# A selective scan cut into tiles of 32 channels x 4 states instead of 64 x 2, with the state sums issued as four 32-column matmuls

## The chip, the cores and the metric

The kernel runs on one core of one Trainium2 chip. A core has five engines that run beside each other[...]: TensorE (PE in the profile, with PEld for its weight loads), VectorE (DVE), ScalarE (ACT), GpSimd (POOL) and SyncE (SP), which here issues most of the DMAs. Each works through its own list of instructions in order. The metric is the device time of one execution in microseconds (us). Times given for the kernel before are the median of three runs, and one further execution was recorded by the profiler.

## The reference

The input is a batch of 8 images of 64 channels and 64 x 64 pixels, in fp32. Four layers follow each other:

- layer 0: attention of all 4096 pixels over each other, a depthwise 3x3 convolution and 1x1 convolutions;
- layer 1: two blocks of window attention (8 x 8 windows, 8 heads) with their MLPs;
- layer 2: a filter that depends on position and image, and a 1x9 convolution;
- layer 3: a selective scan in four directions, then a gated sum of pooled convolutions.

The change is in the scan of layer 3. For every image, each of four directions k, each of 128 channels c and each of 16 states n, with L = 4096 time steps:

```python
def step(h, inp):
    u_t, dt_t, B_t, C_t = inp
    h = h * jnp.exp(dt_t[..., None] * A) + dt_t[..., None] * B_t[:, :, None, :] * u_t[..., None]
    return (h, jnp.einsum('bkcn,bkn->bkc', h, C_t))
```

So each (channel, state) has a first-order recurrence over time, and the output of a channel is the sum over its 16 states of h times C. B and C depend on the state and on time, not on the channel; dt and u depend on the channel and on time, not on the state.

## The kernel before, in words

**Pairs and streams.** The images are handled in four pairs p. For a pair, `front` computes layers 0 to 2 and the sources of the scan (the inputs of the four directions and the gate, written to DRAM), `scans` computes the scan, and `back` does the closing work (normalisation, output projection, pooled convolutions). The front of the first pair runs alone. After that, `scans(p)` runs with `back(p - 1)` and then `front(p + 1)` beside it: these are generators that yield their nominal cost, and after each step of the scan the loop advances them by a share in proportion. With the last pair only `back(2)` and, near its end, `back(3)` are left to stand beside the scan. A scheduler then sets the order of the instructions in each engine's list, within the dependencies; `net.behind` adds one more constraint on order without a semaphore.

**Units and steps.** A unit is one image, one direction and one chunk of 512 time steps (TD); a pair has 64 units. A unit has 128 x 16 = 2048 recurrences of 512 steps. A tile has 128 partitions, so it takes 16 tiles. Before the change a tile holds 64 channels x 2 states (GRP = 2), and a step of the scan handles two tiles (j = 0, 1, the two halves of the channels) with the same two states. A unit has 8 steps.

For each unit, one unit ahead:

- `load` fetches the input xs from DRAM;
- `inputs` computes dt (a matmul into `pdd`, then Exp and Ln on ACT) and the 32 rows of B and C (a matmul into `pbc`), and writes these rows to a DRAM tile `rows`;
- `spread` computes dt times u on DVE (L1735) and spreads dt and dt times u over the states by DMAs from SBUF to SBUF into `du` (L1739): one DMA for each of GRP groups of 128 / GRP channels, each channel's row written to GRP partitions. There are two `du` buffers.

For each step i:

- `fetch` (L1746) brings two rows of B (three steps ahead) and two rows of C (two steps ahead), each row spread over 64 partitions; 256 KB each, four buffers each;
- `products` (L1754, two steps ahead) multiplies B with dt u on POOL into a `vd` buffer of two tiles; there are eight `vd` buffers;
- `step` computes for both tiles the decay `dad` = Exp(dt A) on ACT (L1776) into a PSUM bank, runs the recurrence on DVE (`tensor_tensor_scan`, L1779) into an SBUF tile `hd` or in place into `dad`, keeps the last column for the next chunk on ACT (`carry`, L1787), and multiplies with C into `vd` again: tiles in `hd` on POOL (L1790 both tiles, L1793 one), tiles in `dad` on DVE (L1793). How many of the two tiles DVE takes (`own`) depends on the stage: none and one in turn, or, beside the attention and in the last pair, one, and two at every fourth step. There are two `hd` buffers for even steps and two for odd ones;
- `sums` adds up over the states on PE (L1805): a matmul with the constant `fold` takes the 128 partitions of a tile to 64 channels. The two tiles go to the two halves of the partitions of one PSUM bank `yd`, in which all 8 steps of the unit accumulate. The table `DUE` says after which step a step's sums are issued; it leaves out the step at which `yd` is read;
- `gather` on DVE (L1818 to L1823) adds the finished `yd` into Y at step 2 of the next unit.

All fetches, the spreading DMAs and the loads and stores of the scan stand in one list, SP's.

**Other places that the change touches**, for room in SBUF or with it: `normed` (the buffer `n_sd`), the attention's `e` buffers (L1306), the tile `t1` of layer 2 (L1579 to L1581), and `ge` in the closing work (L1899 to L1902).

Of the kernel before, what the change touches and what calls it, by code (L numbers as in the profile page):

```python
# [9 lines left out]
F32 = mybir.dt.float32  # L10
# [7 lines left out]
P = 128  # L18
# [8 lines left out]
GRP = 2  # L27
# [1132 lines left out]
class _Direct:  # L1160
# [69 lines left out]
    def normed(self, wk, srcs, cen, avg, eps, out_view=None):  # L1230
# [9 lines left out]
        sd = wk.tile([P, CH], F32, name="n_sd", tag="n_sd")  # L1240
# [24 lines left out]
    def layer0(self, p):  # L1265
# [11 lines left out]
        with self.work("w0") as wk:  # L1277
# [10 lines left out]
            for jc in range(NCH):  # L1288
# [9 lines left out]
                for t in range(32):  # L1298
# [6 lines left out]
                    for im in range(2):  # L1305
                        e = wk.tile([P, CH], F32, name="e", tag="e", bufs=6)  # L1306
# [228 lines left out]
    def layer2(self, X):  # L1535
# [11 lines left out]
        with tc.tile_pool(name="w2", bufs=2) as wk:  # L1547
            net.load(wk, (5,))
            cf = net.channel_filters(X, wk, self.pf, "f")
            for c in range(NCH):  # L1550
# [106 lines left out]
    DUE = ((-2,), (-2,), (), (-3,), (-3, -2), (-2,), (-2,), (-2,))  # L1657

    def scans(self, p, beside, cost):
# [39 lines left out]
        for i in (n - 2, n - 1):  # L1699
            self.sums(i, steps[i])  # L1700
# [40 lines left out]
    def fetch(self, i, st, s):  # L1741

        n = NST * s + 2 * (i % 8)
        t = st["BC"[s]] = self.sw.tile([P, TD], F32, name="BC"[s], tag="BC"[s], bufs=4)
        row = self.units[i // 8]["rows"][n : n + 2]
        self.nc.sync.dma_start(t, row.unsqueeze(0).to_broadcast([64, 2, TD]))  # L1746
# [5 lines left out]
    def products(self, i, st):  # L1752
        v = st["v"] = self.sw.tile([P, 2, TD], F32, name="vd", tag="v", bufs=8)
        self.nc.gpsimd.tensor_tensor(v, self.twice(st["B"]), self.units[i // 8]["du"][:, :, 1], ALU.mult)  # L1754

    def step(self, i, st):
# [14 lines left out]
        h = wk.tile([P, 2 - i % 2, TD], F32, name="hd", tag=f"h{i % 2}", bufs=2)  # L1771
        hs = []
        for j in range(2):
            n = n0 + j
            da = self.bank("dad", (P, TD), "da")
            nc.scalar.activation(da, u["du"][:, j, 0], AF.Exp, scale=net.As[:, k, n : n + 1])  # L1776
# [19 lines left out]
    def sums(self, i, st, after=None):  # L1796

        nc, w, net = self.nc, self.w, self.net
        wk, ps = self.sw, self.ps
        u = self.units[i // 8]  # L1800
        k, c = u["k"], u["c"]
        if i % 8 == 0:
            u["y"] = ps.tile([P, TD], F32, name="yd", tag="y", bufs=1)
        for j in range(2):
# [152 lines left out]
```

## Time and profile before

| what | value |
|---|---|
| median of three runs | 12742.49 us (12727.7 to 12745.85) |
| the profiled execution | 12767.64 us |
| its span in the trace | 12765.8 us |
| DMA queue of the scan | 754752 packets, 1510.30 MB, 39.4% of 16 engines' span |
| B and C fetches | 2048 each, 256 KB, 3.6 and 3.5 us from issue to landing |
| du DMAs | 512 of 512 KB, 5.9 us from issue to landing |
| one product on POOL (two tiles) | 2371 ns |
| one scan on DVE | 1267 ns into hd, 1273 ns into dad |
| one decay on ACT | 682 ns |
| one pass of a sum on PE | 738 ns, two passes a matmul, 8192 passes |

How it is read: "busy" is the time in which an engine had an instruction at work. Several of PE's passes can be at work at once, so the mean time of one is more than its share of the time. A group of instructions carries the line of the source and the tiles it writes and reads, as `yd<-vd,pack`. After a group stands the idle time of its engine just ahead of it and what ended that wait. A stretch of the span can be asked for by itself; its row has the length, the busy time and number of PE, PEld, DVE, ACT and POOL, the granted share of the clock of TensorE, the mean busy share of the DMA engines, and GB/s. A row of waits has who waited for whom, the total in us, how many times, and the longest. SPq is the list of DMAs that SP issues.

The stages follow each other in the trace like this: the first pair's front alone up to about 1815 us; the scans of the pairs from there to about 4550, 7475, 10405 and 12520; then the last closing work to the end. Beside the first three scans stand, in this order, the closing work of the pair before (not in the first), the attention of layer 0 of the next pair, its depthwise convolution, its layer 1, its layer 2 and the preparing of its scan's sources.

### The profile page before, as it was taken

How to read it: one execution, taken by the hardware profiler on the slowest of the kernel's cores; microseconds unless marked ns; L12 is line 12 of the kernel's file. 1: busy time of each engine (PE TensorE's matmuls, PEld its weight loads, DVE VectorE, ACT ScalarE, POOL GpSimd, SP SyncE). 2: the span in 40 equal slices, each digit the busy share in tenths (PEclk: the TensorE clock that was granted, in tenths of full speed). 3: DMA queues.
4: the chain of work that ended last, by engine and by line, in shares of the span. 5: the costliest groups of instructions: out<-in, count | busy, mean ns of one | idle time of the engine just before them, and what ended most of it. 6: DMA issues, size and time to landing. Idle time of an engine off the chain costs nothing. (4 is left out here: it accounts for less than half of the span.)

```text
span 12765.8 us, 142485 instructions
## 1 busy us (share of the span) xinstructions
PE 9843.7 (77%) x46358; PEld 3333.1 (26%) x46358; DVE 8687.9 (68%) x10259; ACT 7009.2 (55%) x15693; POOL 7550.7 (59%) x3844
## 2 busy tenths in 40 slices
PE   9888879987887667997888756997888855555556
PEld 2255222223342112222443211222433211111111
DVE  0122256777786776668776679467777679998878
ACT  5533247765663655665665555665566365455444
POOL 0000026677776683667776676467777567777874
PEclk9966779997888778998888877998888967777667
DMA  0000024544443462444443454344444356556554
GB/s 19 1 1 1 6 98 145 150 146 133 133 128 111 145 189 81 138 140 145 125 131 113 128 176 144 93 140 142 126 134 129 100 174 183 170 165 186 171 172 123
DMA packets 779703, 1575.84 MB, mean 123 GB/s; under 512 B 89280, under 2 KB 89408, under 8 KB 778176
## 3 DMA queue, kind: packets, MB, share of 16 engines
q1 hardware_dynamic: 754752, 1510.30, 39.4%
q10 hardware_dynamic: 24192, 56.32, 1.2%
q8 instruction: 367, 6.01, 0.2%
q14 instruction: 392, 3.21, 0.1%
HBM read 1197.16 MB, written 100.66 MB: 102 GB/s over the span
## 5 line engine op out<-in xcount | busy, mean ns | idle before, releaser
L1754 POOL TENSOR_TENSOR vd<-B,du 128x1024 f32<-128x1024 f32 x2048 | 4821.4, 2371 | 3295.1 <-DMA B<-rows 2016.1
L1805 PE MATMUL yd<-vd,pack 128*64 128x512 f32 x8192 | 2946.2, 738 | 933.7 <-POOL vd L1793 595.3
L1776 ACT ACTIVATE dad<-du,As 128x512 f32<-128x512 f32 x4096 | 2733.8, 682 | 1122.5 <-DVE vd L1793 458.5
L1779 DVE TENSOR_TENSOR_SCAN hd<-dad,carry,vd 128x512 f32<-128x512 f32 x1992 | 2497.0, 1267 | 480.0 <-ACT dad L1776 324.4
L1793 POOL TENSOR_TENSOR vd<-hd,C 128x512 f32<-128x512 f32 x1290 | 1659.8, 1290 | 1046.7 <-DVE hd L1779 1030.0
L1779 DVE TENSOR_TENSOR_SCAN dad<-dad,carry,vd 128x512 f32<-128x512 f32 x1592 | 2004.8, 1273 | 166.6 <-ACT dad L1776 164.4
L1790 POOL TENSOR_TENSOR vd<-hd,C 128x1024 f32<-128x1024 f32 x491 | 1158.1, 2359 | 735.5 <-DVE hd L1779 406.6
L1307 ACT ACTIVATE e<-s 128x512 f32<-128x512 f32 x2048 | 1200.2, 591 | 628.3 <-PE s L1301 626.5
L1301 PE MATMUL s<-X 64*128 64x512 f32 x4096 | 1435.8, 646 | 79.6 <-ACT e L1307 58.8
L1805 PEld LDWEIGHTS yd<-vd,pack 128*64 128x64 f32 x8192 | 667.0, 160 | 2815.0 <-issue 1214.6
L1793 DVE TENSOR_TENSOR vd<-dad,C 128x512 f32<-128x512 f32 x1824 | 1207.5, 673 | 239.6 <-ACT carry L1787 232.0
L1293 PE MATMUL po<-e,VT 128*64 128x512 f32 x4096 | 1207.8, 623 | 16.9 <-ACT e L1307 10.2
L1459 PEld LDWEIGHTS w_av<-vals,wide 64*64 64x64 f32 x16384 | 678.1, 173 | 209.7 <-ACT wide L1449 106.3
L1459 PE MATMUL w_av<-vals,wide 64*64 64x9 f32 x16384 | 705.6, 224 | 34.8 <-ACT wide L1449 34.6
L1787 ACT ACTIVATE carry<-hd 128x1 f32<-128x1 f32 (+1 forms) x1559 | 307.6, 200 | 697.1 <-DVE hd L1779 681.0
L1301 PEld LDWEIGHTS s<-X 64*128 64x128 f32 x4096 | 393.4, 186 | 1107.5 <-issue 832.6
L1787 ACT ACTIVATE carry<-dad 128x1 f32<-128x1 f32 x1594 | 268.1, 168 | 698.3 <-DVE dad L1779 688.9
L1717 PE MATMUL pdd<-xs,xdt 128*128 128x512 f32 x512 | 375.7, 824 | 334.6 <-issue 103.1
L1444 DVE TENSOR_TENSOR wide<-w_s,bias 128x512 f32<-128x512 f32 x512 | 327.7, 680 | 254.5 <-PE w_s L1431 246.5
L1449 ACT ACTIVATE wide<-wide 128x512 f32<-128x512 f32 x512 | 309.5, 626 | 318.7 <-DVE wide L1444 194.3
L1239 PE MATMUL pv<-n_sq,pack 128*128 128x512 f32 x576 | 364.5, 718 | 144.0 <-ACT n_sq L1237 130.0
L1316 DVE COPY att<-po 128x512 f32<-128x512 f32 x32 | 21.7, 679 | 643.3 <-PE po L1293 643.3
(246 smaller groups left out, 11137.5 us busy)
## 6 DMA issues: line engine op xcount, KB each, us to landing
B<-rows SPq DMA_DIRECT2D x2048, 256.0 KB, 3.6
C<-rows SPq DMA_DIRECT2D x2048, 256.0 KB, 3.5
du<-du SPq DMA_DIRECT2D x512, 512.0 KB, 5.9
xs<-xt SPq DMA_DIRECT2D x128, 256.0 KB, 3.6
xs<-xc SPq DMA_DIRECT2D x128, 256.0 KB, 3.8
xc<-xcv ACTq DMA_DIRECT2D x64, 256.0 KB, 2.1
zs<-z ACTq DMA_DIRECT2D x64, 256.0 KB, 3.8
xt<-XT ACTq DMA_DIRECT2D x32, 512.0 KB, 4.6
```

Of the source, the lines that this page charges most:

```text
L1293: nc.tensor.matmul(po[half[im]], lhsT=VT[:, t, half[im]], rhs=es[im], start=(t == 0), stop=(t == 31))
L1301: nc.tensor.matmul(ss[im], lhsT=at(half[im], t), rhs=X[half[im], jc * CH : (jc + 1) * CH], start=True, stop=True)
L1307: nc.scalar.activation(e, ss[im], AF.Exp, scale=C**-0.5, accum_out=parts[:, im, t, jc : jc + 1])
L1459: nc.tensor.matmul(self.av[half[im], x % 4 + j, h, :], lhsT=es[h // 4][half[im], j, h % 4, :], rhs=V[half[im], x + j, h, :], start=True, s ...
L1717: nc.tensor.matmul(pd, lhsT=net.xdt[:, k, :], rhs=x, start=True, stop=True)
L1754: self.nc.gpsimd.tensor_tensor(v, self.twice(st["B"]), self.units[i // 8]["du"][:, :, 1], ALU.mult)
L1776: nc.scalar.activation(da, u["du"][:, j, 0], AF.Exp, scale=net.As[:, k, n : n + 1])
L1779: nc.vector.tensor_tensor_scan(along(to), along(da), along(v[:, j]), first, ALU.mult, ALU.add)
L1787: nc.scalar.activation(cs, ends, AF.Copy)
L1790: st["w"] = nc.gpsimd.tensor_tensor(v, h, self.twice(CC), ALU.mult)
L1793: m = engine.tensor_tensor(v[:, j], hs[j], CC, ALU.mult)
L1805: m = nc.tensor.matmul(u["y"][self.HALF[j]], lhsT=w["fold"], rhs=st["v"][:, j], start=(i % 8 == 0), stop=(i % 8 == 7))
```

## The change

A tile of the scan now holds 32 channels x 4 states (GRP = 4), and two steps handle the four channel quarters of the same four states. So a fetch of B or of C brings four rows, each to 32 partitions, and serves two steps; it is made at even steps only, with three buffers each instead of four. `du` has four groups of 32 channels, each spread over four partitions by its own DMA of 512 KB; the tile is twice as large. An even step uses groups 0 and 1, an odd step groups 2 and 3.

A sum takes the 128 partitions of a tile to 32 channels. The sums of two steps are issued together, as four matmuls into the four quarters of the partitions of `yd`, three steps after the even one; `DUE` is gone. The number of matmuls is the same.

There are seven `vd` buffers instead of eight, one `hd` buffer for even steps and one for odd steps instead of two each, one `n_sd` instead of two, five `e` instead of six. `t1` is gone: ACT copies into the place of the result and DVE works on it there. `ge` is gone: the Gelu and the product are made in place in the PSUM bank `pa`.

```diff
-GRP = 2
+GRP = 4
...
-        sd = wk.tile([P, CH], F32, name="n_sd", tag="n_sd")
+        sd = wk.tile([P, CH], F32, name="n_sd", tag="n_sd", bufs=1)
...
-                        e = wk.tile([P, CH], F32, name="e", tag="e", bufs=6)
+                        e = wk.tile([P, CH], F32, name="e", tag="e", bufs=5)
...
-                t1 = wk.tile([P, 8, 64], F32, name="t1", tag="t1", bufs=1)
-                nc.scalar.activation(t1, acc, AF.Copy)
-                nc.vector.scalar_tensor_tensor(a[:, :, 4:68], acc, 0.1, t1, ALU.mult, ALU.max)
+                nc.scalar.activation(a[:, :, 4:68], acc, AF.Copy)
+                nc.vector.scalar_tensor_tensor(a[:, :, 4:68], acc, 0.1, a[:, :, 4:68], ALU.mult, ALU.max)
...
-    DUE = ((-2,), (-2,), (), (-3,), (-3, -2), (-2,), (-2,), (-2,))
...
             if i + 3 < n:
-                self.fetch(i + 3, steps[i + 3], 0)
+                self.fetch(i + 3, steps, 0)
             if 0 <= i + 2 < n:
-                self.fetch(i + 2, steps[i + 2], 1)
+                self.fetch(i + 2, steps, 1)
                 self.products(i + 2, steps[i + 2])
             if i >= 0:
                 self.step(i, steps[i])
-                for j in self.DUE[i % 8]:
-                    if i + j >= 0:
-                        self.sums(i + j, steps[i + j], steps[i]["w"])
+                if i % 2 and i > 2:
+                    self.sums(i - 3, steps, steps[i]["w"])
...
-    def fetch(self, i, st, s):
-
-        n = NST * s + 2 * (i % 8)
-        t = st["BC"[s]] = self.sw.tile([P, TD], F32, name="BC"[s], tag="BC"[s], bufs=4)
-        row = self.units[i // 8]["rows"][n : n + 2]
-        self.nc.sync.dma_start(t, row.unsqueeze(0).to_broadcast([64, 2, TD]))
+    def fetch(self, i, steps, s):
+
+        if i % 2:
+            return
+        n = NST * s + GRP * (i % 8 // 2)
+        t = steps[i]["BC"[s]] = steps[i + 1]["BC"[s]] = self.sw.tile([P, TD], F32, name="BC"[s], tag="BC"[s], bufs=3)
+        row = self.units[i // 8]["rows"][n : n + GRP]
+        self.nc.sync.dma_start(t, row.unsqueeze(0).to_broadcast([P // GRP, GRP, TD]))
...
-        v = st["v"] = self.sw.tile([P, 2, TD], F32, name="vd", tag="v", bufs=8)
-        self.nc.gpsimd.tensor_tensor(v, self.twice(st["B"]), self.units[i // 8]["du"][:, :, 1], ALU.mult)
+        v = st["v"] = self.sw.tile([P, 2, TD], F32, name="vd", tag="v", bufs=7)
+        g = 2 * (i % 2)
+        self.nc.gpsimd.tensor_tensor(v, self.twice(st["B"]), self.units[i // 8]["du"][:, g : g + 2, 1], ALU.mult)
...
-        h = wk.tile([P, 2 - i % 2, TD], F32, name="hd", tag=f"h{i % 2}", bufs=2)
+        h = wk.tile([P, 2 - i % 2, TD], F32, name="hd", tag=f"h{i % 2}", bufs=1)
...
-            nc.scalar.activation(da, u["du"][:, j, 0], AF.Exp, scale=net.As[:, k, n : n + 1])
+            nc.scalar.activation(da, u["du"][:, 2 * (i % 2) + j, 0], AF.Exp, scale=net.As[:, k, n : n + 1])
...
-        for j in range(2):
-            m = nc.tensor.matmul(
-                u["y"][self.HALF[j]], lhsT=w["fold"], rhs=st["v"][:, j], start=(i % 8 == 0), stop=(i % 8 == 7)
-            )
+        m = P // GRP
+        for g in range(GRP):
+            o = nc.tensor.matmul(
+                u["y"][m * g : m * g + m],
+                lhsT=w["fold"],
+                rhs=steps[i + g // 2]["v"][:, g % 2],
+                start=(i % 8 == 0),
+                stop=(i % 8 == 6),
+            )
...
-                ge = wk.tile([P, 8, 64], F32, name="ge", tag="ge", bufs=2)
-                last = nc.scalar.activation(ge, pa, AF.Gelu, bias=w["aggr_b"])
-                nc.vector.tensor_tensor(ge, ge, self.rows(F, c), ALU.mult)
-                nc.vector.tensor_tensor(X[:, cols], X[:, cols], ge.rearrange("p a b -> p (a b)"), ALU.add)
+                last = nc.scalar.activation(pa, pa, AF.Gelu, bias=w["aggr_b"])
+                nc.vector.tensor_tensor(pa, pa, self.rows(F, c), ALU.mult)
+                nc.vector.tensor_tensor(X[:, cols], X[:, cols], pa.rearrange("p a b -> p (a b)"), ALU.add)
```

More of the change, by code (lines that the diff above doesn't have):

```diff
@@ L1698, in scans @@
                 (self.load, self.inputs, self.spread)[i % 8](self.units[i // 8 + 1])
-        for i in (n - 2, n - 1):
-            self.sums(i, steps[i])
+        self.sums(n - 2, steps)
         self.gather(self.units[-1])
@@ L1794, in step, with sums @@
             st.setdefault("w", m)
-    def sums(self, i, st, after=None):
+    def sums(self, i, steps, after=None):
         nc, w, net = self.nc, self.w, self.net
-        wk, ps = self.sw, self.ps
         u = self.units[i // 8]
-        k, c = u["k"], u["c"]
         if i % 8 == 0:
-            u["y"] = ps.tile([P, TD], F32, name="yd", tag="y", bufs=1)
-        for j in range(2):
-            m = nc.tensor.matmul(
-                u["y"][self.HALF[j]], lhsT=w["fold"], rhs=st["v"][:, j], start=(i % 8 == 0), stop=(i % 8 == 7)
-            )
-            if after is not None and j == 0:
-                net.behind(m, after)
+            u["y"] = self.ps.tile([P, TD], F32, name="yd", tag="y", bufs=1)
+        m = P // GRP
[6 more added lines that the diff above has]
+                stop=(i % 8 == 6),
+            )
+            if after is not None and g == 0:
+                net.behind(o, after)
     def gather(self, u):
```

## The prediction

> **What bounds the kernel now.** I read the page first: no engine is full over the span, so the bound changes from stage to stage.
>
> ```profile
> PE 9843.7 (77%) x46358; PEld 3333.1 (26%) x46358; DVE 8687.9 (68%) x10259; ACT 7009.2 (55%) x15693; POOL 7550.7 (59%) x3844
> ```
>
> Then I cut the span by what runs beside the scan (the lines of each stage give the borders) and asked for the busy time of each stretch: attention of layer 0; windows of layer 1; layer 2; the closing work of the pair before; the same in the last pair; the last scans alone.
>
> ```profile
> 5000.00:5835.00 835.00, 806.74 (x2694) 212.15 (x2694) 492.54 (x521) 569.40 (x1662) 475.78 (x255) 0.99 0.42 123
> 6000.00:6880.00 880.00, 761.05 (x6925) 353.89 (x6926) 654.83 (x826) 552.04 (x1066) 657.38 (x321) 0.84 0.43 129
> 6900.00:7200.00 300.00, 258.32 (x665) 86.81 (x664) 183.84 (x220) 106.72 (x212) 172.95 (x85) 0.93 0.34 100
> 7500.00:7950.00 450.00, 270.14 (x591) 72.83 (x592) 394.07 (x437) 229.94 (x448) 335.51 (x163) 0.77 0.51 157
> 10440.00:11540.00 1100.00, 622.40 (x1328) 137.78 (x1330) 996.74 (x1061) 571.14 (x1236) 864.45 (x455) 0.72 0.57 172
> 11560.00:12400.00 840.00, 434.26 (x938) 96.42 (x938) 687.85 (x733) 378.69 (x902) 673.83 (x366) 0.70 0.58 177
> ```
>
> After the length come PE, weight loads, DVE, ACT and POOL busy. PE is the full engine in the first three (97%, 86%, 86%), DVE in the fourth and fifth (88%, 91%); in the last nothing is full (DVE 82%, POOL 80%). The same cuts for the scans alone count two scans a step: 293 in the first, 319 in the second, 419 in the last, so 5.70, 5.52 and 4.01 us a step.
>
> The timeline of PE shows what a sum costs where PE is full:
>
> ```profile
> 5405.45 1.13 PE L1301 MATMUL s<-X 64*128 64x512 f32 x4
> 5406.51 1.08 PE L1293 MATMUL po<-e,VT 128*64 128x512 f32 x4
> 5407.42 1.03 PE L1805 MATMUL yd<-vd,pack 128*64 128x512 f32 x4
> 5408.38 1.12 PE L1301 MATMUL s<-X 64*128 64x512 f32 x2
> ```
>
> Each fp32 matmul is two passes; a group of four records is two matmuls side by side. From s to s this is 2.93 us; the same round without sums (5421.87 to 5423.94) is 2.07. One step's sums cost 0.86 us of PE: two passes of 0.43.
>
> The last stage is held by a queue. One unit (8 steps):
>
> ```profile
> 12017.14 0.68 DVE L1735 TENSOR_TENSOR du<-pdd,xs 128x512 f32<-128x512 f32 x1
> 12026.31 0.51 SPq L1746 DMA_DIRECT2D C<-rows  x1
> 12026.87 0.60 SPq L1746 DMA_DIRECT2D B<-rows  x1
> 12027.57 1.20 SPq L1739 DMA_DIRECT2D du<-du  x2
> 12032.53 1.30 ACT L1776 ACTIVATE dad<-du,As 128x512 f32<-128x512 f32 x2 [7.38 <-DMA du<-du]
> 12033.95 0.69 DVE L1793 TENSOR_TENSOR vd<-dad,C 128x512 f32<-128x512 f32 x1 [6.09 <-ACT carry L1787]
> ```
>
> The next unit's du is ready at 12017.8 but leaves SP at 12027.6: ahead of it stands a C fetch that waits for a buffer, and so for POOL. ACT then idles 7.4 us, DVE 6.1. The waits of 11560 to 12400 add up to:
>
> ```profile
> ACT dad L1776 <- DMA du<-du: 199.4, 41, 9.6
> SPq L1746 <- POOL vd L1793: 230.0, 87, 6.9
> ```
>
> [...]The trace agrees for two halves: the two sums at 5407.42 start at 5407.423 and 5407.429, their second passes at 5407.852 and 5407.858. It has no row with four quarters[...]. [...]po to yd (both 128x64) takes 0.91 start to start, s to po (64x128 to 128x64) 1.06. A switch is worth 0.15 to 0.2 us. [...]I charge each group 0.17.
>
> **The change, part by part.** It is summed on the profiled execution (span 12765.8, whole time 12767.6 us; the median shown is 12742.5, 25 lower).
>
> *Sums.* Per two steps, before: 2 x 0.86 = 1.72 us. After: one group of four, 2 passes x 0.43 + 0.17 = 1.03. That frees 0.345 us of PE a step. In the three attention stages (185 + 147 + 140 = 472 steps by the scans' count) PE is the path, so 472 x 0.345 = 163; DVE there also waits for the unit's last sum (118.1 us in 5120 to 5760), which a shorter PE queue relieves, so I take 180. In layer 1 (483 steps) POOL (75%) and DVE (74%) stand close behind PE, but POOL waits on PE for buffers (118.2 us in 2960 to 3850): bounds 0 and 483 x 0.345 = 167; I take 0.15 a step, 70. In layer 2 (124 steps, DVE 61%) I take 0.3, 37. In the other stages PE has room: nothing.
>
> *Fetches.* B and C go from 16 DMAs of 256 KB a unit to 8; three buffers now hold six steps instead of four. du goes from 2 DMAs of 512 KB to 4. Bytes a unit: 4 + 1 = 5 MB before, 2 + 2 = 4 after. In the new order of SP the du DMAs stand behind a C fetch whose buffer was last read six steps before, so the hold-up of 10 us should go. The first two du DMAs feed even steps, the other two odd ones, so the first step needs no more bytes than now; landing is 5.9 us each, and four issues of 0.6 end 1.2 us later than two. Alone, DVE and POOL need 3.29 and 3.22 us a step of 4.01; with the stall gone I expect 3.6, so 209 x 0.41 = 85. Bounds: 0 (du still late) and 209 x 0.7 = 150. Elsewhere the B waits are hidden behind a full DVE: 0.
>
> *Single hd buffers, seven vd.* The scan of step i+2 now waits until POOL has multiplied step i. Matching each instruction to its step, I asked how often the old run already breaks that rule: in attention 3% of the steps, layer 1 26% (0.56 us a step short), closing work 45 to 57% (1.1 to 1.7), 10440 to 11000 0.64, alone 94% (1.35). Queued behind such a scan on DVE is the work beside it, and ACT's carry copies wait for DVE. Most of it can be paid from slack: POOL's products stand 15 to 20 us ahead of their scans in attention and layer 1 and 4 to 8 in the closing work and alone, so POOL can multiply first. Seven vd with sums in pairs take some 8 to 13 us of that lead, which covers attention and layer 1. I charge 55: 0.3 on the 160 closing steps, the rest on the depthwise part of layer 0, where POOL and DVE are both over 96% busy. Bounds: 0, and the whole shortfall, 483 x 0.56 + 160 x 1.4 + 135 x 0.64 + 209 x 1.35 = about 860.
>
> *The rest.* The new order has 50 fewer activation table loads (1.28 us each by the page's groups, 64 us of ACT) in the stage that prepares the scan's sources, where ACT is 74% and DVE 80%: I take 20, bounds 0 and 64. Five e buffers: the exponential of iteration t reuses a buffer that was read before the scores of t on PE's own queue, nothing. One n_sd: two norms lie at least a whole chunk apart, nothing. t1 in place: the same counts and durations (683 ns on DVE), nothing. ge in PSUM: DVE's two operations on it have both inputs in SBUF now and take 1257 and 1146 ns on average (the add 684 in the median, 2727 at most), while with one input in PSUM the product with C takes 673; so 1.04 us less for each of 24 chunks beside POOL's work, in stages where DVE is full: I take 20, bounds 0 and 25. The first 1815 us (no scan) and the last 250 stay.
>
> Sum: -180 - 70 - 37 - 85 - 20 - 20 + 55 = -357, so 12767.6 - 357 = 12411 profiled and, 25 lower, about 12385.
>
> **The rivals.**
> 1. *The handover takes over (slower).* Place: hd in layer 1, the closing work and alone. Price: up to 860 us against the 55 charged. For: those stages break the rule in a quarter to nine tenths of their steps already. Against: POOL's lead. With a third paid (285) the time is 12615; the change loses once more than (357 + 55) / 860 = 48% is paid; at 60% (515) it ends at 12845.
> 2. *The quarters do not stream four at once.* No row of this trace excludes it. Two at a time: 1.72 + 0.17 = 1.89 a group, +0.085 a step on 1079 PE-heavy steps, 92, less the 70 of the other terms: about 12765. One after another: 3.44 + 0.17 = 3.61, or 0.945 a step more, +1020 - 70: about 13690. The break-even is a group of 1.85.
> 3. *More than I count.* Layer 1 takes the whole 0.345 (97 more) and the alone stage reaches 3.3 (65 more): about 12220. For: sums lag their products by 13 us (median) in layer 1, a sign of PE's backlog. Against: PE's clock is 0.84 there, and less work may lower it.
>
> **How the numbers follow.** My forecast 53%, own range 12240 to 12540; rival 3 15%; rival 1 18% (10 near 12615, 8 near 12845); rival 2 14% (5 near 12765, 9 near 13690). Below 12190 I leave about 6%, above 12880 about 13%. No change is within 0.2% (25 us), about what can be told apart here: half of the two-at-a-time case and edges of rival 1, 6%. Faster: 53 + 15 + 10 less the edges, 76%; slower 18%.
>
> **What would show it.** Right: four sums starting within some 20 ns, two passes of 0.43, PE busy down by 1000 to 1500 us; attention near 4.4 (first pair) and 5.2 us a step; alone near 3.6 with the waits of ACT on du mostly gone; waits of DVE's hd scans on POOL small. Wrong: sums starting 0.4 us apart; DVE hd waiting on POOL for hundreds of us; ACT still waiting on du; layer 1 as long as before, PE at a lower clock.

## The result and the profile after

The changed kernel takes 12826.19 us (median of six runs, 12807.18 to 12846.64), the kernel before 12750.92 us on the same chip: a ratio of 1.0057, with a 95% interval of 1.0043 to 1.0071. So it is slower by some 73 us, where 357 us less were forecast. The profiled execution took 12830.94 us, with a span of 12829.1.

The head of the page and its row for the scans into `hd`, after:

```profile
PE 9326.0 (73%) x46358; PEld 3098.4 (24%) x46358; DVE 8649.5 (67%) x10259; ACT 6922.6 (54%) x15643; POOL 7533.6 (59%) x3844
...
L1777 DVE TENSOR_TENSOR_SCAN hd<-dad,carry,vd 128x512 f32<-128x512 f32 x1992 | 2500.9, 1269 | 854.1 <-ACT dad L1774 316.4
```

The same row of the kernel before:

```profile
L1779 DVE TENSOR_TENSOR_SCAN hd<-dad,carry,vd 128x512 f32<-128x512 f32 x1992 | 2497.0, 1267 | 480.0 <-ACT dad L1776 324.4
```

PE has lost 518 us of busy time, and no engine has gained any. But DVE stands idle 374 us longer just ahead of these scans. ACT ends most of the named idle time in both (324 and 316 us), so the growth has another releaser. The waits over the whole span name it: POOL's products with C, which free `hd`. Before, then after:

```profile
DVE hd L1779 <- POOL vd L1790: 8.3, 6, 1.7
DVE hd L1779 <- POOL vd L1793: 2.1, 2, 1.5
```

```profile
DVE hd L1777 <- POOL vd L1788: 350.2, 169, 9.4
DVE hd L1777 <- POOL vd L1791: 149.5, 104, 4.5
```

That is 500 us instead of 10, one of the signs of being wrong that the prediction named.

The sums' own rows, before and after, show more than PE's total does:

```profile
L1805 PE MATMUL yd<-vd,pack 128*64 128x512 f32 x8192 | 2946.2, 738 | 933.7 <-POOL vd L1793 595.3
```

```profile
L1802 PE MATMUL yd<-vd,pack 128*32 128x512 f32 x8192 | 2051.7, 778 | 648.2 <-POOL vd L1791 312.0
```

Their busy time fell by 895 us, and PE's total by only 518: the passes of its other matmuls take longer, those of the scores 662 ns instead of 646, of `pdd` 871 instead of 824. The granted clock over the span is 0.777 in after and 0.819 in before.

The stretches of after that answer to the six shown of before (length; busy time and instructions of PE, PEld, DVE, ACT, POOL; clock, DMA share, GB/s):

```profile
5006.00:5807.00 801.00, 762.72 (x2697) 183.76 (x2696) 478.05 (x505) 559.27 (x1645) 468.72 (x250) 0.96 0.42 101
6038.00:6975.00 937.00, 757.00 (x6944) 362.77 (x6936) 684.41 (x856) 555.09 (x1084) 691.50 (x338) 0.76 0.43 104
6980.00:7255.00 275.00, 225.72 (x577) 75.35 (x576) 155.70 (x182) 84.44 (x168) 134.78 (x66) 0.86 0.33 80
7540.00:8000.00 460.00, 236.23 (x597) 62.62 (x598) 371.90 (x437) 229.29 (x451) 317.78 (x159) 0.73 0.50 127
10490.00:11610.00 1120.00, 548.51 (x1339) 106.24 (x1337) 982.64 (x1056) 573.45 (x1243) 862.96 (x454) 0.71 0.56 140
11700.00:12480.00 780.00, 396.54 (x938) 61.84 (x934) 685.75 (x728) 373.94 (x910) 677.76 (x367) 0.64 0.61 153
```

The scans in these six rows are 283, 340, 66, 165, 513 and 413. The first row, attention from its first to its last score, takes 801 us where before took 842 (4995 to 5837); that is the gain that was sought, though 283 scans ran beside it instead of 295. Layer 1 (second row) is 81% busy on PE where it was 87%, yet it takes 5.51 us a step, against 5.59 before (853 us from 6053 to 6906, 305 scans; two scans are a step). The last row moves 153 GB/s where before moved 177, but its DMA engines are busier, 0.61 against 0.58. Fewer bytes take more of their time.

PE's timeline, the same place as was shown of before:

```profile
5405.69 1.13 PE L1301 MATMUL s<-X 64*128 64x512 f32 x4
5406.75 1.08 PE L1293 MATMUL po<-e,VT 128*64 128x512 f32 x4
5407.76 1.07 PE L1802 MATMUL yd<-vd,pack 128*32 128x512 f32 x8
5408.76 1.13 PE L1301 MATMUL s<-X 64*128 64x512 f32 x4
```

Eight records, four matmuls of two passes, from 5407.76 to 5408.76: the group costs 1.00 us (forecast 1.03). The single records start at 5407.762, .769, .776 and .782, so four quarters do run at once, 7 ns apart.

The last scans alone, one unit of after:

```profile
12012.53 0.70 DVE L1730 TENSOR_TENSOR du<-pdd,xs 128x512 f32<-128x512 f32 x1
12012.81 0.56 SPq L1743 DMA_DIRECT2D B<-rows  x1
12013.46 7.87 SPq L1734 DMA_DIRECT2D du<-du  x4
12021.44 3.33 SPq L1743 DMA_DIRECT2D C<-rows  x1
12024.81 1.91 SPq L1743 DMA_DIRECT2D B<-rows  x1
12027.96 1.30 ACT L1774 ACTIVATE dad<-du,As 128x512 f32<-128x512 f32 x2 [4.46 <-DMA du<-du]
```

The hold-up ahead of `du` is gone, as forecast: `du` is ready at 12013.23 and leaves SP at 12013.46. But the four issues now take 7.87 us instead of four times 0.6, the next C and B stand behind them, and ACT still waits, until 12027.96. In this unit the third of the four transfers lands at 12027.94. Over all 256 units the fourth issue starts 5.2 us after the first, and the four transfers land 6.9, 9.0, 12.4 and 14.5 us after the first issue (medians); in before the two land after 4.7 and 7.2. The waits of 11700 to 12480:

```profile
ACT dad L1774 <- DMA du<-du: 99.0, 38, 5.3
POOL vd L1752 <- DMA B<-rows: 55.7, 12, 7.6
POOL vd L1752 <- DMA du<-du: 30.4, 19, 3.0
```

This stage went from 4.01 to 3.78 us a step (780 us, 413 scans), not to 3.6.

### The profile page after: what moved, and what is told of

Read it like the earlier page. It is cut to its first block, busy times and chain, and to the rows that moved or that the text cites. A ratio compares the mean times of both kernels' runs of the same rounds, so it can differ in the third digit from the quotient of the medians.

```text
span 12829.1 us, 139155 instructions
## 1 busy us (share of the span) xinstructions
PE 9326.0 (73%) x46358; PEld 3098.4 (24%) x46358; DVE 8649.5 (67%) x10259; ACT 6922.6 (54%) x15643; POOL 7533.6 (59%) x3844
## 3 DMA queue, kind: packets, MB, share of 16 engines
q1 hardware_dynamic: 533568, 1241.76, 39.5%
## 5 line engine op out<-in xcount | busy, mean ns | idle before, releaser
L1802 PE MATMUL yd<-vd,pack 128*32 128x512 f32 x8192 | 2051.7, 778 | 648.2 <-POOL vd L1791 312.0
L1301 PE MATMUL s<-X 64*128 64x512 f32 x4096 | 1492.5, 662 | 117.7 <-ACT e L1307 106.0
L1459 PE MATMUL w_av<-vals,wide 64*64 64x9 f32 x16384 | 757.3, 230 | 47.6 <-ACT wide L1449 47.5
L1459 PEld LDWEIGHTS w_av<-vals,wide 64*64 64x64 f32 x16384 | 727.9, 184 | 240.9 <-ACT wide L1449 114.9
L1802 PEld LDWEIGHTS yd<-vd,pack 128*32 128x32 f32 x8192 | 287.0, 123 | 2059.0 <-issue 767.0
L1431 PE MATMUL w_s<-wide,w_kk 32*64 32x256 f32 x4096 | 458.0, 479 | 41.1 <-DVE wide L1444 29.0
```

The lines of the kernel that those rows point to most:

```text
L1301: nc.tensor.matmul(ss[im], lhsT=at(half[im], t), rhs=X[half[im], jc * CH : (jc + 1) * CH], start=True, stop=True)
L1431: nc.tensor.matmul(ss[g][half[im], j], lhsT=K[rows, 64 * (x + j) : 64 * (x + j) + 64], rhs=qx[rows, x + j], start=True, stop=True,)
L1459: nc.tensor.matmul(self.av[half[im], x % 4 + j, h, :], lhsT=es[h // 4][half[im], j, h % 4, :], rhs=V[half[im], x + j, h, :], start=True, s ...
L1802: o = nc.tensor.matmul(u["y"][m * g : m * g + m], lhsT=w["fold"], rhs=steps[i + g // 2]["v"][:, g % 2], start=(i % 8 == 0), stop=(i % 8 == 6),
```

## The experiments

Each kernel ran beside runs of the kernel before on the same chip. What is compared is its ratio to those; the whole table first, then the questions. "us" is the ratio's distance from 1 times 12741, the median of before in the largest set of runs.

| kernel | ratio to before, 95% interval | us |
|---|---|---|
| after | 1.0057 (1.0043 to 1.0071) | +73 |
| b_hd1: before, one hd each | 1.0225 (1.0203 to 1.0246) | +287 |
| b_pair: before, sums of two steps together | 1.0011 (1.0000 to 1.0021) | +14 |
| b_v7: before, seven vd | 0.9963 (0.9950 to 0.9977) | -47 |
| b_v7pair: before, both of these | 0.9889 (0.9868 to 0.9910) | -141 |
| b_v7pairside: and the edits beside the scan | 0.9863 (0.9843 to 0.9883) | -175 |
| b_quart: b_v7pair with four quarters | 0.9735 (0.9717 to 0.9752) | -338 |
| b_stride2: before, du read from every second partition | 0.9943 (0.9923 to 0.9963) | -73 |
| a_du4r2: after, nothing reads the second half of du | 1.0007 (0.9998 to 1.0015) | +9 |
| a_du2: after, half of du | 0.9868 (0.9844 to 0.9893) | -168 |
| a_du2_hd2: and two hd each | 0.9619 (0.9602 to 0.9636) | -485 |
| a_du2_hd2v8: and eight vd | 0.9605 (0.9584 to 0.9626) | -503 |
| a_strided: after, du read from every fourth partition, wrong channel order | 0.9800 (0.9782 to 0.9819) | -255 |
| a_b2h2: after, two B and C, two hd for even steps | 0.9958 (0.9942 to 0.9975) | -54 |
| a_perm2: after, du read from every fourth partition, complete | 0.9801 (0.9784 to 0.9817) | -254 |
| a_perm2h: a_perm2 with the buffers of a_b2h2 | 0.9657 (0.9641 to 0.9673) | -437 |
| a_perm2v6: a_perm2, two hd each, six vd, three B, two C | 0.9702 (0.9686 to 0.9718) | -380 |

### One hd buffer each

```diff
-        h = wk.tile([P, 2 - i % 2, TD], F32, name="hd", tag=f"h{i % 2}", bufs=2)
+        h = wk.tile([P, 2 - i % 2, TD], F32, name="hd", tag=f"h{i % 2}", bufs=1)
```

> The kernel before with one hd buffer for even and one for odd steps, nothing else. Handover theory (the single hd buffers and the seven vd with paired sums eat the gain): 60 to 120 us slower than before (12810 to 12870), DVE's hd scans wait on POOL for 300 us or more instead of some 10 on the multiplications. du theory (twice the bytes of du, landing later, cost the time) and clock theory (PE with less to do runs at a lower clock and slows layer 1): no change, within 25 us of 12750, clock 0.82.

Measured: 2.25% slower, 287 us, far above the 60 to 120 expected. The page's row of the scans into `hd` gives the size again, 305 us more idle time than before's 480.0, and the waits for POOL's products with C are 450 us instead of 10:

```profile
L1779 DVE TENSOR_TENSOR_SCAN hd<-dad,carry,vd 128x512 f32<-128x512 f32 x1992 | 2499.7, 1269 | 784.6 <-ACT dad L1776 313.1
...
DVE hd L1779 <- POOL vd L1790: 269.3, 114, 6.9
DVE hd L1779 <- POOL vd L1793: 180.8, 116, 4.4
```

A place in layer 1 shows how one such wait travels (timeline of b_hd1, three engines):

```profile
6336.00 6.99 POOL L1754 TENSOR_TENSOR vd<-B,du 128x1024 f32<-128x1024 f32 x3
...
6337.31 2.45 DVE L1779 TENSOR_TENSOR_SCAN hd<-dad,carry,vd 128x512 f32<-128x512 f32 x2
...
6342.93 2.37 POOL L1790 TENSOR_TENSOR vd<-hd,C 128x1024 f32<-128x1024 f32 x1
...
6345.33 1.28 DVE L1779 TENSOR_TENSOR_SCAN hd<-dad,carry,vd 128x512 f32<-128x512 f32 x1 [3.76 <-POOL vd L1790]
...
6346.53 0.73 DVE L1509 SCALAR_TENSOR_TENSOR X<-w_pp,bp,X 128x512 f32<-128x512 f32 x1
...
6347.31 1.19 PE L1431 MATMUL w_s<-wide,w_kk 32*64 32x256 f32 x8 [3.58 <-DVE X L1509]
```

DVE finished both tiles at 6339.76. POOL was in the middle of three early products, one after another in its list, so it multiplied with C only from 6342.93 and freed `hd` at 6345.30. DVE stood 3.76 us; behind that scan in its list was layer 1's `X`, and behind `X` PE stood 3.58 us, in a stage in which PE is busy for 84% of the time. The part of layer 1 from 6142 to 7060 is 918 us for 305 scans, against 853 us for 305 in before.

### Half of du, and the buffers again

In a_du2 only two of the four DMAs of `du` are issued; odd steps take groups 0 and 1 again, so half of the channels is left out; the number of operations of the scan stays. The tile `du` has two groups. The other two give back the buffers in the room that this frees.

```diff
-        for g in range(GRP):
+        for g in range(2):
...
-        g = 2 * (i % 2)
+        g = 0
...
-            nc.scalar.activation(da, u["du"][:, 2 * (i % 2) + j, 0], AF.Exp, scale=net.As[:, k, n : n + 1])
+            nc.scalar.activation(da, u["du"][:, j, 0], AF.Exp, scale=net.As[:, k, n : n + 1])
```

> The kernel after with only two of the four du DMAs; odd steps read the groups of even ones again, so the channels of the upper half get wrong inputs (this part of the result is left out). du theory: 80 us or more faster than after (under 12750), ACT no longer waits for du. Handover and clock theories: within 25 us of after (12826), save up to 30 us in the last scans.

> The changed kernel with two du DMAs only (odd steps use groups 0 and 1 again; half of the channels is left out) and two hd buffers of each size, still seven vd buffers. Stands between 12561 (one hd each) and 12230 (two each, eight vd). Handover theory: the hd buffers are all of it, as in before (where one each cost 285 us): 12230 to 12290. Product-buffer theory: the eighth vd buffer carries at least half, 12380 to 12560.

> As the last, with the room used for two hd buffers of each kind and eight vd as before: quarters and fetches of the change with the old buffers. Handover theory: 150 to 300 us faster than after (12530 to 12680), layer 1 at 5.3 us a step or less. Clock theory: layer 1 still at a clock of 0.76 and no faster than before the change, total 12720 to 12800. du theory: the same time as with the last kernel.

Half of `du` is worth 241 us (1.0057 to 0.9868), two hd each another 317 (to 0.9619), the eighth vd 18, within its uncertainty. The alone stage is at 3.42 us a step in a_du2 (780 us, 456 scans). The clock of TensorE stays low in all of them (0.782, 0.789 and 0.787 over the span, 0.777 in after, 0.819 before) while they are the faster ones, so the low clock does not tell after from the fast ones.

What of the 241 is a wait for the second half, and what is traffic? In a_du4r2 all four DMAs are issued, but odd steps read groups 0 and 1: the last two edits of the diff, with groups 0 and 1 taken from the full tile.

> The changed kernel with all four du DMAs issued, but odd steps read groups 0 and 1 again, so nothing waits for groups 2 and 3. The scan of the other 64 channels is left out in that sense; operations and bytes are those of the change. Of the 265 us that halving du gained (12826 to 12561): traffic theory (four DMAs of 512 KB hold up the list of SP and the fetches of B and C behind them): stays at 12780 to 12830. Late-half theory (the odd steps wait for the second half of du): falls to 12561 to 12620.

64 us go when nothing waits for the second half (1.0057 to 1.0007); 177 (to 0.9868) go only when the DMAs themselves do. Traffic is the larger part.

### Seven vd buffers, sums in pairs, and quarters

```diff
-                for j in self.DUE[i % 8]:
-                    if i + j >= 0:
-                        self.sums(i + j, steps[i + j], steps[i]["w"])
+                if i % 2 and i > 2:
+                    self.sums(i - 3, steps[i - 3], steps[i]["w"])
+                    self.sums(i - 2, steps[i - 2], steps[i]["w"])
...
-        v = st["v"] = self.sw.tile([P, 2, TD], F32, name="vd", tag="v", bufs=8)
+        v = st["v"] = self.sw.tile([P, 2, TD], F32, name="vd", tag="v", bufs=7)
```

> The kernel before with seven vd buffers and the sums of two steps issued together at every second step, still in halves. Handover theory: 40 to 120 us slower than before, POOL's products wait on PE for 1300 us or more (881 before). du and clock theories: within 25 us of before, clock 0.82.

> The kernel before, with one edit: the sums of two steps are issued together after every odd step (still two halves of 64 columns, still eight vd buffers). Before with the same edit and seven vd buffers was 137 us faster than before. Order theory (issuing the sums late and two steps together is what gained: POOL and PE get a smoother order, fewer changes between scores and sums): 12595 or a little less, since the eighth buffer can only help. Buffer theory (the seventh buffer, by holding POOL back, is what gained): near 12735, as before. Rival that the order costs and the buffers gain even more: above 12800.

> The kernel before with seven vd buffers instead of eight and nothing else. Before with eight buffers and the sums of two steps together was no faster than before (12751), with seven buffers and the sums together 137 us faster (12595). Buffer theory (with seven buffers POOL's list puts fewer early products ahead of the products with C, and that alone gains): near 12600. Joint theory (seven buffers help only where sums come late and in pairs, the gain is a chance of the list order): 12700 to 12800. My first charge (fewer buffers cost POOL's lead): above 12760.

Together the two edits gain 141 us where a loss was expected; alone, the pairing gains nothing and the seventh-buffer edit 47. So the parts don't add. The profiles show where the gain falls, the last pair: its first and its last scan are 2141 us apart in before (10504 to 12645, later than the borders given above), 2057 in b_v7 and 2017 in b_v7pair. The other pairs change by 11 us at most, but for the first of b_v7pair (51 less). Beside the last scans alone `du` stood behind a C fetch that waited for POOL, and that hold-up has shrunk. b_v7pair's row of these scans, and ACT's wait:

```profile
11420.00:12200.00 780.00, 439.02 (x978) 96.86 (x976) 712.49 (x763) 399.96 (x937) 684.15 (x371) 0.74 0.64 196
...
ACT dad L1776 <- DMA du<-du: 112.1, 48, 6.3
```

With 428 scans this is 3.64 us a step against 4.01 in before. ACT's wait for `du` was 199.4 us there, in a stretch of 840, and SP's wait for POOL's products with C, 230.0 us there, is 151.8 here. In the last scans `du` leaves SP 9.5 us after it is ready in before, 7.1 in b_v7 and 6.6 in b_v7pair (medians of 26 units). It fits that with a buffer less fewer early products stand ahead of the product with C in POOL's list, so the C buffer comes free sooner; but the scheduler may have moved other instructions as well, and no run separates that.

Then b_quart puts the four sums of two steps into four quarters in this kernel. It takes only the first 32 columns of `fold`, so it sums into the wrong channels; the number, size and order of the matmuls are those of the change.

```diff
-        for j in range(2):
+        for j in range(4):
             m = nc.tensor.matmul(
-                u["y"][self.HALF[j]], lhsT=w["fold"], rhs=st["v"][:, j], start=(i % 8 == 0), stop=(i % 8 == 7)
+                u["y"][32 * j : 32 * j + 32],
+                lhsT=w["fold"][:, 0:32],
+                rhs=steps[i + j // 2]["v"][:, j % 2],
```

> The kernel before with seven vd buffers and the sums of two steps issued together as four quarters of 32 columns, as the change has them; fetches, du, hd and all else as before. It takes only the first 32 columns of fold, so it sums the wrong channels: the amount of work and its order are those of the change, the result is not a scan's. To be set against the same kernel with halves (12595). Quarter theory, as predicted: 0.345 us of PE a step comes free where PE is the path, so another 200 to 290 us less, 12305 to 12395. Rival (after the pairing, the scan's own loop over DVE and POOL is the bound and PE's time is slack): less than 60 us, 12535 to 12595. Clock theory (less work of PE lowers its clock, and the other matmuls stretch): no gain in layer 1, only in the attention, 12480 to 12540, with the clock in layer 1 below 0.78.

```profile
5255.43 1.08 PE L1293 MATMUL po<-e,VT 128*64 128x512 f32 x4
5256.44 1.06 PE L1803 MATMUL yd<-vd,pack 128*32 128x512 f32 x8
5257.43 1.13 PE L1301 MATMUL s<-X 64*128 64x512 f32 x4
```

The quarters alone gain 197 us (0.9889 to 0.9735). The three attention stages, from first to last score, go from 954, 848 and 848 us to 870, 790 and 788: 202 less, as much as the whole gain. In layer 1, the two kernels' rows (b_v7pair, then b_quart):

```profile
6020.00:6880.00 860.00, 752.44 (x6910) 353.81 (x6906) 663.89 (x834) 541.93 (x1050) 662.84 (x323) 0.85 0.44 133
```

```profile
5861.00:6750.00 889.00, 723.56 (x6950) 342.26 (x6942) 693.03 (x863) 558.23 (x1091) 700.76 (x341) 0.77 0.45 136
```

With 322 and 340 scans this is 5.34 and 5.23 us a step: 0.11 gained, the estimate was 0.15. PE's share falls from 87% to 81% and its clock from 0.85 to 0.77. Whether the lower clock took a further part of the gain isn't told by these rows; no run held the clock.

### From which partitions du is read

```diff
-            src = one[m * g : m * g + m].rearrange("c q t -> c (q t)").unsqueeze(1).to_broadcast([m, GRP, 2 * TD])
+            src = one[g : P : GRP].rearrange("c q t -> c (q t)").unsqueeze(1).to_broadcast([m, GRP, 2 * TD])
```

The line is the same in before (GRP = 2, b_stride2) and after (GRP = 4, a_strided). Nothing else changes, so the channels come in a wrong order.

> The changed kernel, with each of the four du DMAs reading every fourth partition of its source (partitions g, g + 4, ...) instead of 32 neighbours. Bytes, number of DMAs and all else are those of the change; the channels come in a wrong order, so the result is not a scan's. Source theory ([...]a DMA of 512 KB takes 8.9 us where 64 partitions took 5.9): landing falls to 6 or 7 us, and most of the 188 us of traffic comes back, 12640 to 12720. Byte theory (2 MB a unit is what it is, whoever holds it): landing near 8.9, 12800 to 12840.

> The kernel before, with each of its two du DMAs reading every second partition of the source instead of 64 neighbours (channels in a wrong order, so no scan's result). Source theory: landing falls from 5.9 us to 4 or 5, the waits of ACT for du in the last scans fall well below 199 us, and the time falls by 30 to 100 us, 12640 to 12710. Rival (there the wait is for the place in the list of SP, not for the transfer): landing may fall, the time stays within 25 us of before.

The page's queue of the scan and its row for `du`: after, a_du2, then a_strided.

```profile
q1 hardware_dynamic: 533568, 1241.76, 39.5%
...
du<-du SPq DMA_DIRECT2D x1024, 512.0 KB, 8.9
```

```profile
q1 hardware_dynamic: 459840, 973.29, 30.2%
...
du<-du SPq DMA_DIRECT2D x512, 512.0 KB, 7.7
```

```profile
q1 hardware_dynamic: 533568, 1241.76, 29.4%
...
du<-du SPq DMA_DIRECT2D x1024, 512.0 KB, 4.6
```

The same bytes from every fourth partition land in 4.6 us instead of 8.9, and the 16 engines spend 29.4% of a shorter span on the queue instead of 39.5%. Four spread DMAs cost the engines less than a_du2's two from neighbours (0.294 x 12488 = 3671 us of the queue, 0.302 x 12562 = 3794). The time falls by 327 us (1.0057 to 0.9800), more than half of `du` was worth; the half that is left in a_du2 is slow too (7.7 us). In before, 64 neighbours took 5.9 us and every second partition takes 4.1; that gains 73 us. There ACT's waits for `du` in the last scans fall only from 199.4 to 145.3 us: `du` still stands 8.7 us in SP's list (in one unit, ready at 12004.8, out at 12013.5), so both the place in the list and the transfer count.

The runs agree that spreading pays (8.9 to 4.6 us, 5.9 to 4.1); why it does, no run shows. Whether 32 and 64 neighbours are alike they answer in two parts. Between the landings of a unit's first and second `du` DMA lie 2.4 us in before and 2.3 in a_du2 (1.4 in a_strided, medians): here the two are alike. But the first lands 4.7 us after its issue in before and 6.9 in a_du2; that is where 5.9 and 7.7 part. What makes it late is open: the two forms also differ in how often a partition is read, twice and four times, and no run separates the two.

### The edits beside the scan

> The kernel before with seven vd buffers, the sums of two steps together (halves), and the four edits beside the scan: one n_sd, five e, t1 and ge in place. Against the same without those four (12595): as predicted, about 20 us for the table loads and 20 for ge, so near 12555. Rival (they lie beside other work): 12580 to 12610.

One `n_sd`, five `e`, `t1` and `ge` in place gain 33 us (0.9889 to 0.9863), where 40 were forecast, though the two intervals overlap. The lines are those of the change's diff.

### Complete kernels

Two hd buffers for even steps fit if B and C have two buffers each:

```diff
-        t = steps[i]["BC"[s]] = steps[i + 1]["BC"[s]] = self.sw.tile([P, TD], F32, name="BC"[s], tag="BC"[s], bufs=3)
+        t = steps[i]["BC"[s]] = steps[i + 1]["BC"[s]] = self.sw.tile([P, TD], F32, name="BC"[s], tag="BC"[s], bufs=2)
...
-        h = wk.tile([P, 2 - i % 2, TD], F32, name="hd", tag=f"h{i % 2}", bufs=1)
+        h = wk.tile([P, 2 - i % 2, TD], F32, name="hd", tag=f"h{i % 2}", bufs=2 - i % 2)
```

> The changed kernel, complete, with two buffers for each of B and C instead of three, and the room given to a second hd buffer for even steps (two there, one for odd steps). Two hd buffers of each size gained 309 us beside half of du. Handover theory: the even steps hand two tiles to POOL and carry at least half of that, so 12600 to 12680, less what two fetch buffers cost. Rival (two fetch buffers of four rows each make B and C late behind the 2 MB of du): 12780 to 12950.

126 us are won (1.0057 to 0.9958), the lower edge of what was expected, and a new wait has come. The waits over the span have two rows that after does not have:

```profile
POOL vd L1791 <- DMA C<-rows: 219.6, 75, 7.4
...
DVE vd L1791 <- DMA C<-rows: 160.5, 92, 5.6
```

I read them as C coming late behind the slow `du` once it has two buffers. By that a quick `du` should be worth more here. To have it in a complete kernel, dt, u and dt u are held in another order of channels: partition 4 m + g has channel 32 g + m. Then the strided read delivers the old order.

```diff
+SPREAD = np.arange(P).reshape(GRP, P // GRP).T.reshape(-1)
...
-    put("drT", f["dtproj_w"].transpose(2, 0, 1))
+    put("drT", f["dtproj_w"].transpose(2, 0, 1)[:, :, SPREAD])
...
-        self.nc.sync.dma_start(x, self.kept[u["image"]][u["k"] % 2][:, u["c"] * TD : (u["c"] + 1) * TD])
+        src = self.kept[u["image"]][u["k"] % 2][:, u["c"] * TD : (u["c"] + 1) * TD]
+        self.nc.sync.dma_start(x, src.rearrange("(g m) t -> m g t", g=GRP))
...
-            nc.vector.scalar_tensor_tensor(yd, self.img(u["x"]), net.dsum, yp, ALU.mult, ALU.add)
+            nc.vector.scalar_tensor_tensor(yd, self.img(u["skip"]), net.dsum, yp, ALU.mult, ALU.add)
```

(The weights xr, xbc and dtb are permuted likewise; the du line is that of a_strided; `skip` is u in the old order, loaded at every fourth unit, and the finished sum goes to a tile of its own.)

> The changed kernel, complete: the channels of dt, u and dt u stand in the order in which partition 4 m + g holds channel 32 g + m, so that each du DMA reads every fourth partition and the results come in the old order. One more DMA of 256 KB at every fourth unit brings u in the old order for the skip term. Source theory: near the run that read every fourth partition in a wrong order (12488), 12480 to 12540, landing 4 to 5 us. Rival (there the order of the channels or what it changed in the data mattered, or the permuted load of xs is slow): 12650 to 12830.

> The same complete kernel, with two buffers for each of B and C and two hd buffers for even steps, one for odd. Beside slow du this exchange gained 146 us (12826 to 12680). If the two losses add: 12480 less 100 to 200, so 12290 to 12390. Rival (the handover was long because B and C came late behind du): less than 60 us, 12430 to 12500.

The last of the three has other buffers:

```diff
-name="BC"[s], tag="BC"[s], bufs=3)
+name="BC"[s], tag="BC"[s], bufs=3 - s)
...
-name="vd", tag="v", bufs=7)
+name="vd", tag="v", bufs=6)
...
-name="hd", tag=f"h{i % 2}", bufs=1)
+name="hd", tag=f"h{i % 2}", bufs=2)
```

> The same complete kernel with two hd buffers of each size, three buffers for B, two for C and six vd buffers instead of seven. Two hd of each size gained 309 us beside half of du, the eighth vd only 22. If the losses add and a sixth buffer does as well as seven: 12180 to 12260. Rival (with six, POOL's products wait for the sums, which come two steps at a time): 12350 to 12500.

a_perm2 is as fast as a_strided (0.9801 and 0.9800): the order of the channels played no part. a_perm2h gains another 183 us, more than the 126 of the same buffers beside slow `du`. It is the best complete kernel: 12307.03 us (12301.83 to 12309.8), 3.4% below before and 4.0% below after. With six vd buffers and all four hd the time is 57 us longer. The page of a_perm2h, and one unit of its last scans:

```profile
L1790 DVE TENSOR_TENSOR_SCAN hd<-dad,carry,vd 128x512 f32<-128x512 f32 x1992 | 2500.1, 1267 | 475.2 <-ACT dad L1787 329.8
```

```profile
11616.92 0.51 SPq L1756 DMA_DIRECT2D B<-rows  x1
11617.49 2.81 SPq L1747 DMA_DIRECT2D du<-du  x4
...
11620.40 1.37 SPq L1756 DMA_DIRECT2D C<-rows  x1
```

The idle time ahead of the hd scans is back to before's (475.2, 480.0). The four issues of `du` take 2.81 us instead of 7.87, and ACT's next scans find `du` there: its waits for it are 11.7 us in the whole span, 123.9 in after. Of a_perm2h's waits for C over the span, none adds up to 9 us.

## Why the prediction was wrong

Two terms failed: "most of it can be paid from slack", which put the single `hd` buffers at 55 us where 317 were measured, and the term for twice the `du` DMAs, put at nothing, where 241 were measured. The runs make a chain from before to after; each row is the difference of two ratios, times 12741.

| part | forecast | measured | from the runs |
|---|---|---|---|
| sums: pairs, seven vd, quarters | -287 | -338 | before to b_quart |
| fetches by four, edits beside the scan | -125 | -147 | b_quart to a_du2_hd2 |
| one hd each | +55 | +317 | a_du2_hd2 to a_du2 |
| twice the du DMAs | 0 | +241 | a_du2 to after |
| sum | -357 | +73 | |

The rows hold for this order. Beside other edits the same buffers are worth other amounts: one `hd` each costs 287 us in before, and a second one for even steps, paid with a buffer each of B and C, gains 126 beside slow `du` and 183 beside quick `du`. The row of the fetches already has two `du` DMAs that read 32 neighbours each.

- **Sums: right in mechanism; that the row comes near is in part luck.** That four quarters run at once was an assumption of the forecast that no row of before showed. In after they do: the group costs 1.00 us, its four matmuls start 7 ns apart, so rival 2 is out. Of the 338 us the quarters are 197, in attention 202 (forecast 180 for these stages); layer 1 gains 0.11 us a step against the 0.15 taken. The other 141 are from pairs and seven buffers, which the forecast had only as a cost; they fall mostly in the last pair, where the forecast expected its gain from the fetches. In after itself attention is just 88 us shorter than before (936, 842, 827 to 913, 801, 803). With half of `du` (a_du2) it takes 879, 782 and 788, so 68 us of its gain are lost to the second two DMAs. So two signs of being right stayed out: attention takes 4.60 us a step in the first pair and 5.66 in the second (b_quart: 4.39 and 5.40, forecast 4.4 and 5.2), and PE's busy time fell by 518 us, not by 1000 to 1500.
- **Fetches: the stall went, as forecast, and another came.** The row's nearness is luck too: of the 147 us 33 are the edits beside the scan, and by the profiles of b_quart and a_du2_hd2 the last pair has some 50 (2018 to 1969 us from its first scan to its last), and the forecast had put the fetches at nothing elsewhere. The C fetch ahead of `du` no longer holds SP. With `du` halved the last scans run at 3.42 us a step, below the 3.6 forecast. The step that failed here is "the first step needs no more bytes than now; landing is 5.9 us each, and four issues of 0.6 end 1.2 us later than two". Landing is 8.9 us, so even the first two transfers are in only 9.0 us after the first issue instead of 7.2, the second half after 14.5; the four issues took 7.87 us of SP in the unit shown, and B and C stood behind them. The duration of before was carried over to a DMA that reads half as many partitions, each twice as often; no row of before showed that form, so it needed bounds on both sides, and it had none. The runs afterwards separate it: 177 us of traffic, 64 of waiting for the second half.
- **Single hd: the bound held, the value in it was far too low.** "Most of it can be paid from slack" failed: 317 us, or 287 in before alone, are 33 to 37% of the 860 us bound, about the "third paid" of rival 1. POOL's lead over the scans is no slack for the products with C: in the place shown, the early products that make up the lead stand ahead of the product that frees `hd`, and it starts at 6342.93 though its tiles are there from 6339.76 on. Attention, which breaks the rule in 3% of its steps, lost nothing in b_hd1 (933, 839, 832 us against 936, 842, 827), layer 1, for which nothing was charged, lost 50 to 66 us each time (929, 921 and 908 against 878, 855 and 858, from the first window score to the first matmul into layer 2's `acc`).
- **Rival 1** named the handover and layer 1 rightly, but not the last scans, where 94% of the steps break the rule: from the last pair's first scan to its last b_hd1 takes 2142 us, before 2141. (There `du` left SP 4.9 us late in b_hd1, not 9.5, which may hide a loss.) And alone it would not have turned the sign: 317 us are below its break-even of 48% of 860. It took both terms.
- **Rival 3's doubt**, that less work of PE may lower its clock, agrees with layer 1: the clock is 0.76 with PE 81% busy in after, 0.83 with 87% in before. That the one causes the other is not shown. It does not explain the loss: a_du2_hd2 and a_perm2h have 0.79 over the span, near after's 0.777 and below before's 0.819, and are 3.8% and 3.4% faster than before. What the lower clock costs all of these kernels is not known, as no run held it.

## What to carry to other kernels

Lead on an engine that works through a list need not be slack (here 317 us were lost where 55 were charged): before a buffer is taken away, look at what stands in that list between the last use and the instruction that frees it. In these runs a DMA's duration went with its form, the partitions it reads included (512 KB landed in 4.1 to 8.9 us); when a change narrows its source, bound the new duration instead of carrying the old one over, and try to spread the source over the partitions, which was worth 327 us in after and 73 in before. When fewer bytes give a higher DMA share, as here 0.58 at 177 GB/s and 0.61 at 153, look for a transfer whose form has got worse.

## What the runs showed that was not expected

- The same 512 KB from SBUF to SBUF land in 8.9 us from 32 neighbouring partitions, in 4.6 from every fourth; in before 5.9 from 64 neighbours, 4.1 from every second.
- SP's own issues took longer where the transfers were slow: four of `du` took 7.87 us with neighbours and 2.81 spread, in the units shown. The fourth starts 5.2 us after the first in after and 2.2 in a_strided (medians).
- A buffer less can be faster: seven vd buffers gain 47 us, and 141 with sums in pairs, which gain nothing by themselves; most of it in the last pair, where `du` left SP sooner.
- The clock of TensorE in layer 1 fell from 0.85 to 0.77 when PE's share there fell from 87% to 81%, and the time per step still went down, from 5.34 to 5.23 us.
